# Layer 3's way back to its queries turned on TensorE, bias rows as products, and a different order around the choice

## The chip, the cores and the metric

The kernel runs on one core of one Trainium2 chip. Its time is the device time of one execution in microseconds, as the median of a few runs. The core has five engines with a queue of their own: TensorE (PE, with its weight loads as PEld), VectorE (DVE), ScalarE (ACT), GpSimd (POOL) and SyncE (SP), which issues most of the DMAs. Each works through its queue in order and waits on semaphores for the others.

## The reference

Four layers of gated cross-attention, each followed by a feed-forward part, on eight batches of 256 tokens with 128 features, in f32:

```python
x = x + tanh(g_xattn[l]) * L{l}_xattn(layernorm(x), ctx)      # l = 0 .. 3
x = x + tanh(g_ffn[l]) * L{l}_ffn(layernorm(x))
```

All attentions have 16 heads of 8 features. Layers 0 to 2 are full ones (2 causal). Layer 2's FFN is a mixture of 8 experts (2 per token) and a shared one. Layer 3 matters most here:

```python
q_norm = q / norm(q);  k_norm = k / norm(k)
mean_scores = einsum('bhqd,bhkd->bhqk', q_norm, k_norm).mean(-1)
_, top_idx = top_k(mean_scores, 51)                  # per head
q_sel = take_along_axis(q, top_idx)
attn = softmax(q_sel @ k.T / sqrt(8));  ctx_sel = attn @ v
context = zeros(...).at[bidx, hidx, top_idx].set(ctx_sel)
out = context.reshape(Bq, 256, 128) @ Wo.T + bo
```

So per head 51 of 256 queries attend, and their results go back to their places among 256. Layer 3's FFN quantizes its input to a grid of 6-bit numbers by blocks of 32, and multiplies by a quantized weight, plus a bias.

## The kernel before

The order of all work is written out by hand. A list of "beats" holds, for each beat, jobs in a fixed order (`beat(...)`) and jobs that `put` fits in by a rough cost per engine or `force` sets by number. At the end `plan_.run()` issues them beat by beat, so every engine's queue follows the beats. `one_bank()` hands out the eight banks of PSUM in turn: a new one waits until its last user eight banks ago is done.

Layers 0 to 2 interleave attention steps with the FFN of the layer before. The change touches three later places.

**The end of layer 2's attention** (the ten beats from `d`). The last batches are normed, routed to experts (`route2`: `logits`, `best`, `only`, `before_`, `index`, `label`, `send`) and scattered to DRAM by POOL. `shared_hidden` and `shared_project` (the shared expert, four pieces each per pair of batches) fill in. `shared_project(blk, 0)` first turns `cmb`, the weights of the experts ("codes"), into `cmbT` by four products (L1024) and a copy on ACT (L1028), and then uses it in a product of 8 rows (L1035) that adds the experts' biases. After these beats `tabulate` gives the table of tiles, SP fetches weights and rows, and 39 expert tiles follow (`tile_turn` L961, `tile_hidden` L975, `tile_project` L1001).

**The choice** (beats from `beats3b`). The experts' results are added (`combine`, L1058), each pair of batches is normed (`stats`, `first`, `steps_`, `apply`; four pairs, the first three with Newton steps on POOL, the last on DVE, `apply` L308 on ACT) and turned (`turn_norm`, L326/L327). `square_queries` (L1133, L1135) squares the projected queries. `lengths` (L1144, `reciprocal` L1148) and `cosines` (L1155, L1160 to L1162) of two pairs at a time give the rank numbers `sc` for all heads and batches at once. `choose` takes the 51 greatest of each row with seven rounds of `max`, numbers them 1 to 51 in `gt` (`order_`, L1199/L1200), sends `gt` to DRAM (`places3`, L1201), and `spread` turns it into `chosen` (L1207/L1208).

**Layer 3** (`PLACE3`). One beat per step `i`; each name in the list is issued for batch `i + k`:

- `one_hot` (L1258, DVE): a table of 128 x 1632, 1 where a query is the u-th chosen one; `gather` (L1283, PE) multiplies the projected queries (`query_rows`) by it.
- `scores3` (L1299), `maxima3` (L457, DVE), `lower3` (L1311, a copy on ACT and a DMA `k<-nT` L1316 of the negated maxima), `weights3` (L1325, exponentials on ACT L1332), `values3` (L1343), `turn3` (L1353 and three DVE operations): the softmax of the 51 queries of each head.
- `fetch_places` (L1249): two DMAs of 512 KB from `places3`, each row broadcast to 64 partitions; `one_hot_back` (L1253, DVE) compares the 128 x 2048 values with the lane's number. `spread3` (L1376, PE) multiplies the results by this table.
- `output` (`add_to_x`: L530 brings x into a bank by the identity, L532 adds the product, ACT copies it back, L535); the bias row `ob` is added by POOL (`bias`, `add_row` L331). `vals` adds the value bias in two POOL operations (L390).
- Layer norm (`stats` .. `apply`) with Newton steps on POOL (L265 to L268, `m` L298/L299), the grid FFN (`scales` .. `sized`, split over DVE and POOL), `turn_`, `out_` (again `add_to_x`, then the DMA out), with its bias row `frow` added by POOL (`add_row`). Batches 6 and 7 do these on DVE.

Of the kernel before, what the change touches and what calls it, by code (L numbers as in the profile page):

```python
# [88 lines left out]
def tile_gated_cross_attention_stack(ctx: ExitStack, tc: tile.TileContext, ins: dict, out: bass.AP):  # L89
# [182 lines left out]
    def layer_norm(bs, row=None, eng=None, out_eng=None, lag=2, wait=1):  # L272

        n = len(bs)
        eng = eng or G
        got = {}

        def stats(k):
            if k == 0:
                got["mv"] = tiny("mv", [P, 4, 2])[:, 0 : 2 * n, :]  # L280
            st, mv = tiny("st", [P, 2, 6]), got["mv"]
            for i in range(2):
                V.bn_stats(st[:, i, :], xs[:, 2 * bs[k] + i, :])
                V.bn_aggr(mv[:, 2 * k + i, :], st[:, i, :])

        def first():
            v = tiny("v", [P, 4])[:, 0 : 2 * n]
            V.tensor_scalar(v, got["mv"][:, :, 1], LN_EPS, None, ALU.add)
            got["y"] = *guess(v, 2 * n, f"ln{n}"), v

        def steps_():
            y, t_, v = got["y"]
            newton(y, t_, v, eng)
            m = tiny("m", [P, 4])[:, 0 : 2 * n]
            if eng is V:
                V.scalar_tensor_tensor(m, got["mv"][:, :, 0], -1.0, y, ALU.mult, ALU.mult)  # L296
            else:
                eng.tensor_tensor(m, got["mv"][:, :, 0], y, ALU.mult)  # L298
                eng.tensor_scalar(m, m, -1.0, 0.0, ALU.mult, ALU.add)  # L299
            got["m"] = m  # L300

        def apply(k):
            t = norm[bs[k]] = moe.tile([P, 2, ROW], F32, tag="xn", name="xn", bufs=8)
            for i in range(2):
                c = slice(2 * k + i, 2 * k + i + 1)
                o, x, y, m = t[:, i, 0:D], xs[:, 2 * bs[k] + i, :], got["y"][0][:, c], got["m"][:, c]
                if out_eng is A:
                    A.activation(o, x, AF.Identity, bias=m, scale=y)  # L308
                else:
                    eng.tensor_scalar(o, x, y, m, ALU.mult, ALU.add)  # L310

        e = "V" if eng is V else "G"
        todo = [(1, dict(V=0.7), stats, k) for k in range(n)]
        todo += [(1, dict(V=0.5), first), (1, {e: 2.8 if eng is G else 1.9}, steps_)]
        todo += [
            ((wait if eng is G else 1) if k == 0 else 1, dict(A=0.7) if out_eng is A else {e: 0.9}, apply, k) for k in range(n)
        ]
        todo += [(lag if k == 0 else 0, dict(T=0.45, A=0.37), turn_norm, b) for k, b in enumerate(bs)]
        if row is not None:
            todo += [(0, dict(G=0.73), add_row, b, row) for b in bs]  # L320
        return todo
# [55 lines left out]

    def vals(l, b):
        ps = one_bank()
        for c in range(2):  # L380
            nc.tensor.matmul(
                ps[:, c * P : (c + 1) * P], lhsT=ctxT[:, b * S + c * P : b * S + (c + 1) * P], rhs=wvo[:, l, 0, :],
                start=True, stop=True,
            )
# [3 lines left out]
        if l == NL - 1:  # L388
            for c in range(2):
                G.tensor_tensor(o[:, c], o[:, c], bv3.rearrange("p (h d) -> p h d", d=HD), ALU.add)  # L390
# [136 lines left out]
    def add_to_x(b, xT, w):  # L527

        px, xb = one_bank(), xs[:, 2 * b : 2 * b + 2, :].rearrange("p t d -> p (t d)")
        nc.tensor.matmul(px[:, 0:S], lhsT=ident, rhs=xb, start=True, stop=False)  # L530
        for c in range(2):
# [5 lines left out]
    def output3(b):  # L537
        add_to_x(b, cts.pop((NL - 1, b)), wvo[:, NL - 1, 1, :])
# [479 lines left out]

    def shared_project(blk, i):
        t, hT = 4 * blk + i, shared[blk]  # L1020
        if i == 0:
            ps = one_bank()
            for k in range(4):
                nc.tensor.matmul(  # L1024
                    ps[0:NE, k * P : (k + 1) * P], lhsT=cmb[:, 4 * blk + k, :], rhs=ident, start=True, stop=True
                )
            cT = work.tile([P, 512], F32, tag="sy", name="cmbT", bufs=2)[0:NE, :]
            A.copy(cT, ps[0:NE, :])  # L1028
            shared[blk, "c"] = cT
# [107 lines left out]
    def lengths(ms):  # L1137
# [3 lines left out]
        o, ps = slice(32 * ms[0], 32 * ms[0] + 64), one_bank()  # L1141
# [6 lines left out]
        V.reciprocal(rank3["sc"][o], ps[o, 0:S])  # L1148

    def cosines(ms):  # L1150

        o, ps = slice(32 * ms[0], 32 * ms[0] + 64), one_bank()
        for k in range(2):
            for m in ms:
# [3 lines left out]
                )  # L1158
        sc, size = rank3["sc"][o], rank3["size"][o]
# [4 lines left out]
    def choose():  # L1164
# [31 lines left out]
        def order_():  # L1196
# [4 lines left out]
            nc.sync.dma_start(out=places3[:, :], in_=gt)  # L1201
# [20 lines left out]
    places3 = dram.tile([P, S], F32, tag="places3", name="places3")  # L1222
# [3 lines left out]
    def area(b):  # L1226
# [4 lines left out]
            o[:, 256:512].rearrange("p (g s u) -> p g s u", g=2, s=2),  # L1231
        )

    def clear_area(r, i):
        q, a, u = area(r)
        if i == 0:
            G.memset(q, 0.0)
        else:
            G.memset(a, 0.0)
            G.memset(u, 1.0)  # L1240

    def fetch_places(b):
# [3 lines left out]
        o = a3[b, "back"] = a3["back"][:, b % 2].rearrange("p (k q) -> p k q", q=S)  # L1246
        src = places3[b * H : (b + 1) * H, :].rearrange("(k s) q -> s k q", s=2)
        for s in range(2):
            nc.sync.dma_start(out=o[64 * s : 64 * s + 64], in_=src[s].unsqueeze(0).to_broadcast([64, 8, S]))  # L1249

    def one_hot_back(b):
        o = a3[b, "back"]
        V.tensor_scalar(o, o, lane64, None, ALU.is_equal)  # L1253

    def one_hot(b):
# [5 lines left out]
        )  # L1261

# [10 lines left out]
    def gather(b):  # L1273
        q, a, _ = area(b)
        o = a3.pop((b, "to"))
# [59 lines left out]
    def values3(b):  # L1335
# [11 lines left out]
        A.copy(area(b)[2][:, :, :, 0:U], ps[:, 0 : 4 * U].rearrange("p (g s u) -> p g s u", g=2, s=2))  # L1347

    def turn3(b):
        u = area(b)[2]  # L1350
        pt = one_bank()
        for g in range(2):
            nc.tensor.transpose(pt[:, g * P : (g + 1) * P], u[:, g].rearrange("p s u -> p (s u)"), ident)  # L1353
        pt = pt[:, 0:S].rearrange("p (k e) -> p k e", e=32)
        rd, own = tiny("rd3", [P, 8]), tiny("own3", [P, 8, 2])
        V.reciprocal(rd, pt[:, :, HD])
        V.tensor_tensor(
            own, rd.unsqueeze(2).to_broadcast([P, 8, 2]), own_half.unsqueeze(1).to_broadcast([P, 8, 2]), ALU.mult
        )
        shape = [P, 8, 2, HD]  # L1360
        V.tensor_tensor(
            ctx3(b)[:, :, 0 : 2 * HD].rearrange("p k (s d) -> p k s d", s=2),
# [6 lines left out]
    def spread3(b):  # L1369
# [3 lines left out]
        for i in range(2):  # L1373
            for j in range(4):
                k = 2 * j + i
                nc.tensor.matmul(  # L1376
                    pt[strip(j), 0:S], lhsT=x[:, 32 * k - 16 * i : 32 * k - 16 * i + 32], rhs=back_[:, k, :],
# [80 lines left out]
    def ffn3(b, eng=None):  # L1458
# [9 lines left out]
        def out_():  # L1468
            xb = xs[:, 2 * b : 2 * b + 2, :]
            add_to_x(b, got["rT"], w3T)  # L1470
# [9 lines left out]
        (-1, "turn3"), (0, "lower3 bias"), (-2, "apply"), (2, "one_hot"), (1, "gather"), (-1, "spread3"), (1, "fetch_places"),  # L1480
        (0, "weights3"), (-1, "output"), (-4, "out_"), (-3, "off add_row"), (-2, "scales units_"), (0, "one_hot_back"), (-3, "lower_ sized"), (1, "scores3"),
        (-2, "step scale_"), (0, "values3"), (-1, "stats first steps_"), (-2, "near"), (1, "vals"),
# [64 lines left out]
    own_head = own2 = head_rows = u51 = lane64 = own_rows = own_half = bq3 = every = None  # L1547

    def more_constants():
        nonlocal prior, region, first, tiles, lane, token2, nowhere, taken, ident16, mask16, own_head, own2, head_rows  # L1550
        nonlocal u51, lane64, own_rows, own_half, bq3, every
# [25 lines left out]
        for m in range(NB // 2):  # L1577
# [3 lines left out]
        u51, lane64 = count("u51", [P, TOP_QUERIES], [[1, TOP_QUERIES]], 1), count("lane64", [P, 1], [[1, 1]], 1, 1)  # L1581
        upper = shaped("upper", [P, 1], 0.0, (None, [[0, 1]], ALU.is_ge, -64.0, 63, -1))
        G.tensor_tensor(lane64, lane64, upper, ALU.add)
        own_half = shaped(
            "own_half", [P, 2], 1.0, (lambda t: t[:, 0:1], [[0, 1]], ALU.is_ge, 0.0, 63, -1),
            (lambda t: t[:, 1:2], [[0, 1]], ALU.is_ge, 0.0, -64, 1),
# [78 lines left out]
    for base in (  # L1665
        (last(1),), (fill[0][0], last(3)), (fill[0][1], last(5)), (fill[0][2], last(7), fill[0][3]),
        ((keys, 3, 0), (keys, 3, 1)), ((keys, 3, 2),), (fill[0][4],), (fill[0][5],),
        ((keys, 3, 3), (square, 0), fill[0][6], (square, 1), fill[0][7], (squares, 0), fill[1][0]),
# [33 lines left out]
    for i in range(TILES + 2):  # L1702
# [20 lines left out]
        {p[2].__name__ + str(p[3] if p[2].__name__ in ("apply", "stats") else ""): p[2:] for p in layer_norm(pair, ob[:, 3, :], G if m in (0, 1, 2) else V, A)}  # L1723
# [16 lines left out]
    for base in (  # L1740
        [(take, b) for b in range(NB)] + h2 + joins(0, V), p2[0:2] + statistics(0), p2[2:4] + h3 + joins(1, V),
        statistics(1) + joins(2, V) + p3[0:2] + applied(0), turned_(0) + statistics(2) + p3[2:4] + applied(1) + [(square_queries, 0)],
        turned_(1) + joins(3, V) + [(square_queries, 1)], statistics(3), applied(2), turned_(2) + applied(3) + [(square_queries, 2)],
        [(lengths, (0, 1)), (cosines, (0, 1))], turned_(3) + [(square_queries, 3)],
        [(lengths, (2, 3)), (cosines, (2, 3))],
# [11 lines left out]
    for b in range(NB):  # L1757
        eng = G if b < 6 else V
        for p in last_norm((b,), frow[:, 1, :], eng, A) + ffn3(b, eng):
            what[p[2].__name__, b] = p[2:]  # L1760
        for f in (
            query_rows, one_hot, one_hot_back, fetch_places, gather, scores3, maxima3, lower3, weights3, values3, turn3, spread3
        ):
            what[f.__name__, b] = f, b
        what["bias", b] = add_row, b, ob[:, NL - 1, :]
        what["vals", b], what["output", b] = (vals, NL - 1, b), (output3, b)
    first = [(f, b) for b in range(2) for f in ("fetch_places", "query_rows", "one_hot")]
# [76 lines left out]
```

## Time and profile before

| | |
|---|---|
| median of 3 runs | 872.11 us (871.02 to 877.95) |
| the profiled execution's own time | 872.14 us |
| its span | 870.4 us |
| mean granted TensorE clock | 0.933 of full speed |
| busy PE, DVE, ACT, POOL | 776.4, 640.5, 444.3, 387.9 us |
| expert tiles | about 603 to 697 us of the span |
| `choose` and `spread` | about 732 to 743.6 us |
| layer 3's attention and FFN | 743.6 us to the end |

A line of the timeline gives start, length, engine, source line, operation, out<-in by the program's names, shapes (partitions x elements), how often, and in brackets the engine's idle time before it and what ended that. A line of the chain of waits gives start, length and what held the end up. An f32 product shows as two MATMULs, a transpose as one; PE's lengths overlap, so the spacing of starts tells what one costs in a stream.

### The profile page before, as it was taken

What the parts mean: (1) busy time and instruction counts of PE and PEld (TensorE: products, weight loads), DVE (VectorE), ACT (ScalarE), POOL (GpSimd) and SP (SyncE); (2) the same over time, 40 slices, a digit from 0 to 9 for tenths busy, and PEclk for the clock granted to TensorE, in tenths of its full rate; (3) what the DMA queues carried; (4) which work ended last, traced back from release to release, by engine and by line L of the source; (5) the groups of instructions that cost most, each with busy time, mean ns of one, the idle gap of its engine ahead of it and who ended that gap; (6) DMA issues with size and microseconds to landing.
All of it is one profiled execution on the core that took longest, in us unless ns stands there. A gap on an engine that the chain in (4) does not pass through costs nothing.

```text
span 870.4 us, 23085 instructions
## 1 busy us (share of the span) xinstructions
PE 776.4 (89%) x8682; PEld 555.2 (64%) x8682; DVE 640.5 (74%) x1972; ACT 444.3 (51%) x1111; POOL 387.9 (45%) x1022
## 2 busy tenths in 40 slices
PE   4999999999999999999999998859999995587775
PEld 2666667666766666666776676535998861465553
DVE  7978889898886578767656675746687576578886
ACT  2567777777776522222665563635455542354442
POOL 3425478777433205022522235574455540048771
PEclk7999999999999999999999996978999996698885
DMA  4314333222220000010100100324576330553430
GB/s 121 103 52 101 86 86 93 62 66 64 65 56 3 1 1 1 2 24 2 27 15 15 27 10 21 110 80 126 145 201 184 94 96 0 104 100 75 87 63 24
DMA packets 59758, 56.40 MB, mean 65 GB/s; under 512 B 7112, under 2 KB 48912, under 8 KB 59648
## 3 DMA queue, kind: packets, MB, share of 16 engines
q1 hardware_dynamic: 56944, 50.06, 22.9%
q0 software_dynamic: 2272, 4.72, 1.5%
q8 instruction: 69, 1.13, 0.6%
q14 instruction: 41, 0.34, 0.1%
q10 hardware_dynamic: 432, 0.15, 0.1%
HBM read 31.99 MB, written 15.16 MB: 54 GB/s over the span
## 4 chain that ended last, share of the span: by engine, by line
PE 66%; DVE 22%; ACT 4%; issue 4%; POOL 3%; DMA 2%; another core or an unknown queue 0%; SPq 0%; DVEq 0%; ACTq 0%
PE one L405 17%; PE one L485 8%; DVE nm L457 7%; PE one L745 4%; PE one L734 4%; PE one L735 4%; PE one L975 4%; PE one L1001 4%; PE one L342 3%; PE one L394 2%; PE one L1032 2%; PE one L521 1%; ACT e L460 1%; PE one L1014 1%; DVE back L1253 1%
## 5 line engine op out<-in xcount | busy, mean ns | idle before, releaser
L457 DVE TENSOR_REDUCE nm<-one 128x2 f32<-128x512 f32 (+1 forms) x416 | 240.6, 642 | 85.3 <-PE one L394 42.9
L460 ACT ACTIVATE e<-one 128x512 f32<-128x512 f32 (+1 forms) x384 | 185.9, 566 | 59.9 <-PE one L405 58.5
L405 PE MATMUL one<-q,k 32*128 32x256 f32 (+1 forms) x1536 | 191.1, 381 | 5.4 <-issue 1.6
L405 PE MATMUL one<-k,q 32*128 32x256 f32 (+1 forms) x1536 | 185.3, 387 | 3.2 <-DMA q<-proj 3.2
L405 PEld LDWEIGHTS one<-k,q 32*128 32x128 f32 x1536 | 133.3, 193 | 36.1 <-issue 15.2
L405 PEld LDWEIGHTS one<-q,k 32*128 32x128 f32 x1536 | 139.1, 189 | 16.2 <-issue 5.4
L485 PE MATMUL one<-e,vaug 128*32 128x256 f32 (+1 forms) x1536 | 87.3, 369 | 1.0 <-ACT e L460 0.9
L411 POOL TENSOR_SCALAR_AFFINE_SELECT e<-e 128x1024 f32<-128x1024 f32 x32 | 35.0, 1094 | 96.2 <-ACT e L460 80.4
L265 POOL TENSOR_TENSOR t_ln<-y_ln 128x2 f32<-128x2 f32 (+1 forms) x105 | 21.4, 204 | 104.0 <-DVE y_ln L255 98.5
L485 PEld LDWEIGHTS one<-e,vaug 128*32 128x32 f32 x1536 | 45.2, 111 | 33.8 <-DVE nm L457 5.1
L980 ACT ACTIVATE h<-one,tb 128x128 f32<-128x128 f32 x156 | 44.6, 370 | 41.2 <-PE one L975 36.9
L785 POOL DMA_INDIRECT done<-y,back_to x39 | 39.5, 1014 | 48.2 <-DVE xT L963 27.5
L737 ACT ACTIVATE act<-one 128x512 f32<-128x512 f32 x40 | 23.9, 597 | 61.0 <-PE one L734 56.0
L745 PEld LDWEIGHTS one<-ffn,act 128*128 128x128 f32 x320 | 41.2, 192 | 16.7 <-issue 14.1
L738 DVE TENSOR_TENSOR act<-act,one 128x512 f32<-128x512 f32 x40 | 27.4, 685 | 25.8 <-PE one L735 18.7
L491 ACT COPY u<-one 128x256 f32<-128x256 f32 x48 | 17.9, 374 | 48.9 <-PE one L485 48.4
L975 PE MATMUL one<-xT,k 128*128 128x128 f32 x312 | 41.5, 276 | 1.0 <-DVE xT L963 1.0
L308 ACT ACTIVATE xn<-xs,m,y_ln 128x128 f32<-128x128 f32 x64 | 27.7, 487 | 26.9 <-DVE m L296 17.2
L745 PE MATMUL one<-ffn,act 128*128 128x128 f32 x320 | 41.4, 275 | 0.0
L734 PE MATMUL one<-xnT,ffn 128*128 128x512 f32 x80 | 41.3, 598 | 0.0
L1001 PE MATMUL one<-w2all,h 128*128 x312 | 41.2, 276 | 0.0
L735 PE MATMUL one<-xnT,ffn 128*128 128x512 f32 x80 | 40.9, 592 | 0.0
(346 smaller groups left out, 1571.1 us busy)
## 6 DMA issues: line engine op xcount, KB each, us to landing
k<-in_w_dram SPq DMA_DIRECT2D x39, 256.0 KB
sent<-zero SPq DMA_DIRECT2D x34, 264.0 KB
back<-places SPq DMA_DIRECT2D x16, 512.0 KB
k<-proj SPq DMA_DIRECT2D x24, 128.0 KB
q<-proj SPq DMA_DIRECT2D x48, 64.0 KB
xt<-sent SPq DMA_DIRECT2D x39, 66.0 KB
w2all<-in_w_dram SPq DMA_DIRECT2D x4, 512.0 KB
yt<-done SPq DMA_DIRECT2D x8, 256.0 KB
```

Source lines behind the costliest of these rows:

```text
L405: nc.tensor.matmul(o, lhsT=a, rhs=r, start=alone_ or s == 0, stop=alone_)
L411: G.affine_select(d, d, pattern=[[0, 8], [1, P]], compare_op=ALU.is_ge, fill=0.0, base=0, channel_multiplier=-1)
L457: V.tensor_reduce(nm, ps.rearrange("p (s k) -> p s k", s=2), AX.X, ALU.max, negate=True)
L460: A.activation(e, ps[:, 0 : 2 * w].rearrange("p (s q) -> p s q", s=2), AF.Exp, scale=SCALE)
L485: nc.tensor.matmul(ps[strip(j), q0:S], lhsT=va[:, at : at + 32], rhs=e[:, c, j, s, 0 : S - q0], start=c == 0 and s == 0, stop=c == 1 and s ...
L734: nc.tensor.matmul(pa, lhsT=wa, rhs=toks, start=True, stop=True)
L735: nc.tensor.matmul(pb, lhsT=wb, rhs=toks, start=True, stop=True)
L745: nc.tensor.matmul(py[:, i * P : (i + 1) * P], lhsT=a[:, i * P : (i + 1) * P], rhs=w, start=n == 0, stop=n == len(ws) - 1,)
L785: i = G.indirect_dma_start(out=dst[:, :], out_offset=bass.IndirectOffsetOnAxis(ap=rows_, axis=0), in_=src, in_offset=None)
L975: nc.tensor.matmul(ps[:, ch * P : (ch + 1) * P], lhsT=wa[:, ch * P : (ch + 1) * P], rhs=turned[i][0], start=True, stop=True)
L980: A.activation(h[:, ch, :], ps[:, ch * P : (ch + 1) * P], AF.Gelu, bias=plan["tb"][:, i, ch : ch + 1])
L1001: nc.tensor.matmul(ps[:, 0:D], lhsT=h[:, ch, :], rhs=wb[:, ch, :], start=ch == 0, stop=ch == NCH - 1)
```

## The change

1. `places3`, `fetch_places` and `one_hot_back` go. `turn_places(b, i)` makes the table of the way back from the gathering one: per batch 16 transposes of 128 x 102 on PE, into four banks, and four copies of 102 x 512 on ACT. `turn3` and `spread3` work on 102 partitions in place of 128, and `one_hot` moves in `PLACE3` from the front to between `step scale_` and `stats`, with the transposes in two halves around `scores3`. Before the loop only batch 0's `query_rows` and `one_hot` are made.
2. The three bias rows of layer 3 are products of a row of ones (one partition) with the row, accumulated into the bank that is filled anyway (`row_to`): in `vals`, `output3` and `out_`. POOL's additions go.
3. The codes of the first shared block (`shared_codes(0)`) are turned three beats earlier; pieces of the shared expert move by one beat or within one.
4. `lengths` and `cosines` are split from `inverse` and `ranked`; the first pairs' products stand ahead of the last turnings, and the last pair's second batch is normed on DVE (`vector_too`).

```diff
-                if out_eng is A:
+                if out_eng is A and k not in vector_too:
                     A.activation(o, x, AF.Identity, bias=m, scale=y)
...
+    def row_to(ps, row, start=False):
+        nc.tensor.matmul(
+            ps[:, 0:S].rearrange("p (c d) -> p c d", c=2), lhsT=ones[0:1, 0:P],
+            rhs=row[0:1].unsqueeze(1).to_broadcast([1, 2, D]), start=start, stop=False,
+        )
     def vals(l, b):
+        last = l == NL - 1
+        if last:
+            row_to(ps, bv3, True)
...
-        if l == NL - 1:
-            for c in range(2):
-                G.tensor_tensor(o[:, c], o[:, c], bv3.rearrange("p (h d) -> p h d", d=HD), ALU.add)
...
-    def add_to_x(b, xT, w):
+    def add_to_x(b, xT, w, row):
         nc.tensor.matmul(px[:, 0:S], lhsT=ident, rhs=xb, start=True, stop=False)
+        row_to(px, row)
...
+    def shared_codes(blk):
...
-        if i == 0:
+        if i == 0 and (blk, "c") not in shared:
+            shared_codes(blk)
...
-            nc.sync.dma_start(out=places3[:, :], in_=gt)
...
-    def fetch_places(b):
...
-        for s in range(2):
-            nc.sync.dma_start(out=o[64 * s : 64 * s + 64], in_=src[s].unsqueeze(0).to_broadcast([64, 8, S]))
-    def one_hot_back(b):
-        V.tensor_scalar(o, o, lane64, None, ALU.is_equal)
+    def turn_places(b, i):
+        o, t = a3[b, "to"], a3["back"][0 : 2 * U, b % 2].rearrange("p (k q) -> p k q", q=S)
+        for k in range(4 * i, 4 * i + 4, 2):
+            ps = one_bank()
+            for m in range(2):
+                for c in range(2):
+                    at = (2 * m + c) * P
+                    nc.tensor.transpose(
+                        ps[0 : 2 * U, at : at + P],
+                        o[:, c, 2 * (k + m) : 2 * (k + m) + 2, :].rearrange("p s u -> p (s u)"), ident,
+                    )
+            A.copy(t[:, k : k + 2, :].rearrange("p k q -> p (k q)"), ps[0 : 2 * U, :])
...
     PLACE3 = (
-        (-1, "turn3"), (0, "lower3 bias"), (-2, "apply"), (2, "one_hot"), (1, "gather"), (-1, "spread3"), (1, "fetch_places"),
-        (0, "weights3"), (-1, "output"), (-4, "out_"), (-3, "off add_row"), (-2, "scales units_"), (0, "one_hot_back"), (-3, "lower_ sized"), (1, "scores3"),
-        (-2, "step scale_"), (0, "values3"), (-1, "stats first steps_"), (-2, "near"), (1, "vals"),
+        (-1, "turn3"), (0, "lower3"), (-2, "apply"), (1, "gather"), (-1, "spread3"),
+        (0, "weights3"), (-1, "output"), (-4, "out_"), (-3, "off"), (-2, "scales units_"), (1, "turn_places0"), (-3, "lower_ sized"), (1, "scores3"),
+        (-2, "step scale_"), (0, "values3"), (1, "turn_places1"), (2, "one_hot"), (-1, "stats first steps_"), (-2, "near"), (1, "vals"),
         (2, "query_rows"), (-3, "turn_"), (1, "maxima3"),
     )
...
-        (last(1),), (fill[0][0], last(3)), (fill[0][1], last(5)), (fill[0][2], last(7), fill[0][3]),
-        ((keys, 3, 0), (keys, 3, 1)), ((keys, 3, 2),), (fill[0][4],), (fill[0][5],),
-        ((keys, 3, 3), (square, 0), fill[0][6], (square, 1), fill[0][7], (squares, 0), fill[1][0]),
+        (last(1),), (fill[0][0], last(3)), (fill[0][1], last(5)), (fill[0][2], (shared_codes, 0), last(7), fill[0][3]),
+        ((keys, 3, 0), (keys, 3, 1)), ((keys, 3, 2),), (fill[0][4], fill[0][5]), (fill[0][6],),
+        ((keys, 3, 3), (square, 0), (square, 1), fill[0][7], fill[1][0], (squares, 0)),
...
-        turned_(1) + joins(3, V) + [(square_queries, 1)], statistics(3), applied(2), turned_(2) + applied(3) + [(square_queries, 2)],
-        [(lengths, (0, 1)), (cosines, (0, 1))], turned_(3) + [(square_queries, 3)],
-        [(lengths, (2, 3)), (cosines, (2, 3))],
+        turned_(1) + joins(3, V) + [(square_queries, 1)], statistics(3) + applied(2), [(lengths, (0, 1)), (cosines, (0, 1))],
+        applied(3) + turned_(2) + turned_(3) + [(inverse, (0, 1)), (ranked, (0, 1)), (square_queries, 2), (square_queries, 3)],
+        [(lengths, (2, 3)), (cosines, (2, 3)), (inverse, (2, 3)), (ranked, (2, 3))],
...
-    first = [(f, b) for b in range(2) for f in ("fetch_places", "query_rows", "one_hot")]
+    first = [("query_rows", 0), ("one_hot", 0)]
```

## The prediction

> **What bounds the kernel now.** I read the page first, then the stretches from 560 us on (the layers before them are cut into the same instructions by both kernels), then the timeline there.
>
> ```profile
> PE 776.4 (89%) x8682; PEld 555.2 (64%) x8682; DVE 640.5 (74%) x1972; ACT 444.3 (51%) x1111; POOL 387.9 (45%) x1022
> ```
>
> TensorE (PE) is 89% busy overall, but not where the change lies. Layer 3 works on one batch after the other, some 13 us each. In two of those stretches (length, then PE, PEld, DVE, ACT and POOL busy, granted clock, DMA share, GB/s):
>
> ```profile
> 786.30:799.54 13.24, 11.07 (x230) 8.33 (x220) 11.54 (x26) 5.86 (x18) 10.68 (x24) 0.74 0.41 82
> 799.54:812.80 13.26, 10.73 (x237) 8.29 (x228) 11.57 (x27) 6.14 (x19) 10.70 (x24) 0.87 0.42 91
> ```
>
> VectorE (DVE) does 11.6 of 13.26 us and GpSimd (POOL) 10.7, so the pace is set by the two together. The timeline of one batch shows how (start, length, engine, instruction, idle time before it):
>
> ```profile
> 799.54 1.89 DVE L1258 TENSOR_TENSOR to<-chosen,u 128x1632 f32<-128x1632 f32 x1
> 799.80 1.68 POOL L298 TENSOR_TENSOR m<-mv,y_ln 128x2 f32<-128x2 f32 x1
> 801.80 0.88 ACT L308 ACTIVATE xn<-xs,m,y_ln 128x128 f32<-128x128 f32 x2 [2.09 <-POOL m L299]
> 802.71 0.42 DVE L1400 TENSOR_REDUCE q_scl<-xn 128x8 f32<-128x256 f32 x1 [1.28 <-ACT xn L308]
> 803.90 1.83 DVE L1253 TENSOR_SCALAR back<-back,lane 128x2048 f32<-128x2048 f32 x1
> ```
>
> POOL's tiny `m`, elsewhere 0.20 us, lasts 1.68 and ends with `one_hot` (L1258): the two get in each other's way. The ring is: y_ln on DVE (796.39), Newton steps on POOL, `m`, `xn` on ACT, L1400 at 802.71 (6.3 later), then 6.9 of DVE work with L1253 in it to the next y_ln at 809.64. PE meanwhile:
>
> ```profile
> 812.28 0.28 PE L1311 MATMUL one<-ident,nm 128*8 128x128 f32 x1 [1.29 <-DVE nm L457]
> ...
> 813.30 1.07 PE L1376 MATMUL one<-back,zero 128*32 128x256 f32 x16
> 814.76 1.15 PE L1325 MATMUL one<-k,keys 32*128 32x102 f32 x32 [0.39 <-DMA k<-nT]
> 815.85 0.70 PE L530 MATMUL one<-xs,ident 128*128 128x256 f32 x2
> 817.37 0.71 PE L532 MATMUL one<-wvo,cT 128*128 128x128 f32 x4 [0.83 <-ACT cT L1381]
> 817.92 0.60 PE L530 MATMUL one<-xs,ident 128*128 128x256 f32 x2
> 818.36 0.61 PE L532 MATMUL one<-w3T,rT 128*128 128x128 f32 x4
> 818.89 1.15 PE L1299 MATMUL one<-keys,k 32*128 32x256 f32 x16
> ...
> 823.90 0.41 PE L1353 MATMUL one<-ident,k 128*128 128x128 f32 x2 [1.70 <-DVE nm L457]
> 825.61 0.38 PE L1311 MATMUL one<-ident,nm 128*8 128x128 f32 x1 [1.29 <-DVE nm L457]
> ```
>
> From start to start the pieces of this batch come to 8.8 us at nearly full clock (1.0 to L1376, 1.0, 1.1, 0.6, 0.55, 0.45, 0.55, 1.1, then 0.85 values, 0.55 `vals`, 0.45 queries, two times 0.3 turning); the rest of 13.3 is waiting. So PE has 4.5 us to spare per batch.
>
> Two places ahead of the loop also hold PE:
>
> ```profile
> 582.69 0.79 PE L1035 MATMUL one<-b,cmbT 8*128 8x128 f32 x2 [7.83 <-ACT cmbT L1028]
> ...
> 711.24 1.16 PE L1032 MATMUL one<-w,hT 128*128 128x128 f32 x8
> 712.33 0.48 PE L1035 MATMUL one<-b,cmbT 8*128 8x128 f32 x2
> ```
>
> ```profile
> 719.26 1.65 ACT L308 ACTIVATE xn<-xs,m,y_ln 128x128 f32<-128x128 f32 x4
> 721.42 1.92 PE L1144 MATMUL one<-qsq,head_sum 128*32 128x256 f32 x8
> 724.98 1.01 PE L326 MATMUL one<-ident,xn 128*128 128x128 f32 x4
> ```
>
> At 574.9 PE stops for 7.8 us until ACT, busy with the labels of batch 6, comes to copy the codes. At 721 the last pair's normed rows are ready, but their turning (724.98) stands behind `lengths` and `cosines` of the first pairs.
>
> **The change, part by part.** Times are set against the profiled execution: 872.14 us, of which 870.4 is the span. The median of the runs is 872.11, so the sum carries over.
>
> *Codes ahead.* The copy now stands before ACT's labels, so batch 7's turning no longer waits for L1035. ACT still copies the labels first (to 581.6) and one projection (0.68), then xnT: 582.2 in place of 584.14, 1.9 earlier. DVE's choice of experts and the table follow it. One `shared_project` (1.7 us, L1032 and L1035 from 591.86) also leaves the stretch before the first tile turns at 602.96; what that gives is limited by the rows' DMA, issued at 598.88. Ends 1.9 and 3.4; I take **-2.5**. The codes' four products (1.0 us of PE) now stand ahead of batch 7's last product; DVE reads that only at 570.79 and not before 568.8, so they are covered, and would cost 1.0 otherwise.
>
> *Choice.* `lengths` and `cosines` of the first pairs (1.85 + 1.7 us) run while DVE does the last statistics, and two of the last four `xn` go to DVE (0.3 each instead of 0.41 in ACT's row). The last turning then waits for `xn` (719.8) and not for 724.98. With the four turns, copies and two L1133 behind each other, `lengths` of the last pairs ends near 725.2 at full clock (729.4 now), 726.7 at the clock of L1144's row: -2.7 to -4.2, **-3.4**. The `reciprocal` of the first pairs (1.75) still ends before the second begins.
>
> *Tables.* Removed per batch: L1253 (1.82 on DVE), two DMAs of 512 KB on SP's queue, two `add_row` (0.73 each) and two `vaug` additions (0.43 each) on POOL. Added on PE: 16 transposes and three one-row products; on ACT four copies of 102x512, bounded by 0.56 (8x512 copy) and 0.69 (128x512 activation), so 2.4, with 6 of 13 us used so far: covered.
>
> A transpose: the pairs of L1353 and L1464 show 0.11 us of spacing (L1353's row: 0.41 for two, 0.27 of it the last one's own latency); 16 make 1.8. The price is bounded above by that latency, 0.27.
>
> A one-row product of 256 columns: L530's spacing (817.92 to 818.36) gives 0.44. The nearest row with few partitions is L1035: 0.41 for 128 columns where full products take 0.22, and the L1032 group behind it takes 1.09 where it takes 0.89 at 613.33. So 0.4 more: 0.83, and three make 2.5. 0.44 is the lower end. *TensorEngine Tiling (Array Packing)* of the Trainium skill, Tiling Modes, Key Properties, says that changing the tiling mode drains TensorE. By it each of the three products pays on both sides; without it the sum below would be 5.9 us lower (the first rival). L1035's rows agree with it.
>
> PE per full batch: 8.8 + 1.8 + 2.5 + 0.4 (weights wait for `nT`'s DMA) = **13.5**. The ring on DVE, POOL and ACT: L1253's 1.8 leaves the second part and `one_hot` (1.9) enters it, between `step` and the statistics, 7.1; in the first part `m` is no longer held up (-1.5): 4.9. Together **12.0**. `one_hot` now holds POOL's `scale_` instead, which is needed only after statistics and `first` (1.9 us later). So PE takes over the pace, 0.2 above today's.
>
> Batch by batch (from L1311 to L1311; today 12.7, 9.6, 12.0, 13.25, 13.25, 13.3, 11.85): before the first, PE does 16 transposes and one product more, partly under the wait for `k`: +0.7. Batch 0 loses the wait below, but PE's longer queue takes most of it: -0.9.
>
> ```profile
> 752.18 4.80 DMA k<-nT
> ```
>
> (4.80 behind the tables' transfers; 1.65 at 764.88.) Batch 1, which has little else: 11.3, +1.7. Batch 2: 11.4, -0.6. Batch 3, no output of the FFN yet: PE 11.7, the ring 12.0, -1.25. Batches 4 and 5: +0.2, +0.1. Batch 6, whose `one_hot` and queries are gone: 13.0, +1.1. Batch 7 has no transposes left and L1253 is gone, 1.8, and 0.5 of the lead that DVE has from batch 6: -2.3. At the end two products stand on the chain where the clock is low (L530's second piece takes 0.86 to 1.0 at 865.27 and 851.94): +2.0; the POOL additions that they replace were hidden there.
>
> Sum: -2.5 - 3.4 + 0.7 - 0.9 + 1.7 - 0.6 - 1.25 + 0.2 + 0.1 + 1.1 - 2.3 + 2.0 = -5.15. **867.0 us.**
>
> **Rivals.**
>
> *The ring sets the pace (0.26).* The one-row products pay no switch (0.44), so PE needs 12.3 per full batch. Some 15 products count on the path, 0.39 each: 5.9 less, **861.1**. For it: they are accumulations into a bank already open. Against it: L1035 is one too, and pays.
>
> *The gains ahead of the loop are swallowed (0.2).* The expert stage starts when rows arrive, not when PE is free, and `choose` when DVE is done: half of 5.9 is lost and the loop costs one more: **871**. For it: between 577.44 and 579.43 DVE waits for something that the trace calls unknown, which the change leaves.
>
> *Transposes don't overlap (0.1).* Each costs its latency, 0.27, not 0.11: 2.6 us more per batch, on PE's queue, which is the bound from 0.1 each on. Batches -1 to 6, one of them half covered: 7 x 2.4 = 17 us: **884**, slower. Against it: four L326 at 709.35 let the next product start at 709.84. *TensorE: Matmul & The Clock Gate* (Part 4: PE-mode transpose) gives about 275 ns for one in a kernel; the row's 0.27 is the same figure, but as latency, not as spacing. By that figure as a spacing the sum would be this rival's.
>
> That the change does not do what it says I see no case for: the transposes and products stand in the changed queue.
>
> **How the numbers follow.** The forecast has 0.44, with 863.5 to 870.5 as its own range. The ends of the terms (start 1.9 to 3.4, choice 2.7 to 4.2, products 0.44 to 0.83) and the first two rivals span 860 to 872; I reach to 876 for part of the third. 1%, 8.7 us, is about what a measurement can tell from no change here (its runs reach from 871.02 to 877.95). Below 863.4: the first rival and a little of the forecast, 0.31. Above 880.8: 0.09. Between: 0.60.
>
> **What would show it.** Right: L1253 gone; PE over 12.5 of 13.5 us busy in the full batches at a clock near 1.0; POOL's `m` at 0.2; the pace near 13.5 and unchanged; `nT`'s DMA below 2.5 us in batch 0; no wait of 7.8 us for `cmbT`; the first tile turned near 600.5, `chosen` near 737.5. Wrong: batches of 12 us with PE idle before L457's releases (then the products are cheap), or above 15 (then the transposes are dear); `chosen` at 742 or later.

## The result, and the profile after

The changed kernel takes 868.78 us (median of 20 runs, 863.34 to 872.79) and the kernel before 872.02 (20 runs): ratio 0.996, 95% interval 0.9943 to 0.9978. In a later set of runs, beside the kernel before on the same chip, it was 0.9938 (0.9922 to 0.9954). It is a little faster, by less than 1%, as forecast. The profiled run took 870.73 us with a span of 867.9.

Its page, first line (to be held against PE 89%, DVE 74% and POOL 45% before):

```profile
PE 805.0 (93%) x8858; PEld 571.9 (66%) x8858; DVE 622.5 (72%) x1966; ACT 460.4 (53%) x1141; POOL 363.5 (42%) x984
```

The full batches 4 and 5, by stretch (length, then PE, PEld, DVE, ACT and POOL busy, granted clock, DMA share, GB/s):

```profile
792.98:806.08 13.10, 12.73 (x242) 9.42 (x241) 9.23 (x24) 8.48 (x24) 8.94 (x23) 1.00 0.05 13
806.08:819.18 13.10, 12.72 (x242) 9.40 (x241) 9.23 (x24) 8.35 (x24) 7.71 (x19) 1.00 0.05 13
```

They are 13.10 long where they were 13.25, but another engine fills them: TensorE works for 12.7 us where it worked for 10.7 to 11.1, VectorE has gone from 11.6 to 9.2. TensorE's timeline of the second of them:

```profile
806.08 0.39 PE L1329 MATMUL one<-ident,nm 128*8 128x128 f32 x2
...
808.52 1.15 PE L1343 MATMUL one<-k,keys 32*128 32x102 f32 x32 [0.38 <-DMA k<-nT]
809.61 0.70 PE L537 MATMUL one<-xs,ident 128*128 128x256 f32 x2
810.24 0.69 PE L380 MATMUL one<-ob,ones 1*128 1x256 f32 x2
810.86 0.71 PE L540 MATMUL one<-wvo,cT 128*128 128x128 f32 x4
811.41 0.60 PE L537 MATMUL one<-xs,ident 128*128 128x256 f32 x2
811.93 0.69 PE L380 MATMUL one<-frow,ones 1*128 1x256 f32 x2
812.56 0.71 PE L540 MATMUL one<-w3T,rT 128*128 128x128 f32 x4
813.11 1.04 PE L1274 MATMUL one<-ident,to 128*102 128x128 f32 x8
814.07 1.15 PE L1317 MATMUL one<-keys,k 32*128 32x256 f32 x16
```

L380 is `row_to`, L1274 the transposes of `turn_places`, L1329 is `lower3` (L1311 before). The only wait is 0.38 us for `nT`'s DMA; no piece waits for VectorE any more. Eight transposes take 0.96 to 1.02 us from start to start, 0.12 to 0.13 each.

The batches in the order of the prediction (first `lower3` to the next, and at last to `spread3` of batch 7): 10.0, 11.3, 11.2, 11.4, 13.1, 13.1, 16.3, 10.9. The 16.3 is a disturbance of this one trace: from 824.6 to 831.5 us the granted clock was 0.5, and a second trace of the same kernel (below) has 13.2 there. That second trace stands for batch 6 and for the length of the loop in what follows.

### The profile page after: what moved, and what is told of

It is laid out like the page before. It is cut to its first block, busy times and chain, and to the rows that moved or that the text cites. A ratio compares the mean times of both kernels' runs of the same rounds, so it can differ in the third digit from the quotient of the medians.

```text
span 867.9 us, 23365 instructions
## 1 busy us (share of the span) xinstructions
PE 805.0 (93%) x8858; PEld 571.9 (66%) x8858; DVE 622.5 (72%) x1966; ACT 460.4 (53%) x1141; POOL 363.5 (42%) x984
## 4 chain that ended last, share of the span: by engine, by line
PE 72%; DVE 16%; DMA 4%; ACT 3%; issue 2%; POOL 1%; another core or an unknown queue 1%; SPq 0%; DVEq 0%; ACTq 0%; POOLq 0%
PE one L412 17%; PE one L492 8%; DVE nm L464 6%; PE one L753 4%; PE one L742 4%; PE one L743 4%; PE one L983 4%; PE one L1009 3%; PE one L342 3%; PE one L1274 2%; PE one L380 2%; PE one L401 2%; PE one L1043 1%; PE one L540 1%; DMA k<-nT 1%
## 5 line engine op out<-in xcount | busy, mean ns | idle before, releaser
L464 DVE TENSOR_REDUCE nm<-one 128x2 f32<-128x512 f32 (+1 forms) x416 | 240.5, 640 | 91.2 <-PE one L401 42.9
L412 PEld LDWEIGHTS one<-q,k 32*128 32x128 f32 x1536 | 138.7, 189 | 16.1 <-issue 5.1
L492 PE MATMUL one<-e,vaug 128*32 128x256 f32 (+1 forms) x1536 | 87.2, 369 | 1.0 <-ACT e L467 0.9
L492 PEld LDWEIGHTS one<-e,vaug 128*32 128x32 f32 x1536 | 45.2, 111 | 33.8 <-DVE nm L464 5.1
L283 DVE BATCH_NORM_STATS2 st<-xs 128x6 f32<-128x128 f32 x128 | 34.6, 270 | 7.4 <-ACT xs L543 6.9
```

Source lines behind the costliest of these rows:

```text
L412: nc.tensor.matmul(o, lhsT=a, rhs=r, start=alone_ or s == 0, stop=alone_)
L464: V.tensor_reduce(nm, ps.rearrange("p (s k) -> p s k", s=2), AX.X, ALU.max, negate=True)
L492: nc.tensor.matmul(ps[strip(j), q0:S], lhsT=va[:, at : at + 32], rhs=e[:, c, j, s, 0 : S - q0], start=c == 0 and s == 0, stop=c == 1 and s ...
```

## The experiments

One reading goes through all of them. The stretch from layer 2's end to the first expert tile varied by up to 12 us between traces whose code is the same up to there, so a trace is cut at two marks: the start of layer 2's last values product (L492, L485 before) and the end of the copy into `chosen`. What lies behind the second mark repeats to a few tenths where the clock is the same. The runs were made on different chips, on which the kernel before has medians from 866.9 to 875.3 us, so times are compared as ratios to it on the same chip. In us:

| kernel | layer 2's last values to chosen | chosen to first lower3 | a full batch | chosen to end of span | time to before, with interval |
|---|---|---|---|---|---|
| before | 184.9 | 7.9 | 13.25 | 126.8 | |
| changed, first trace | 180.4 | 10.0 | 13.10 | 128.9 | 0.996 (0.9943 to 0.9978) |
| changed, second trace | 175.2 | 9.2 | 13.12 | 126.0 | 0.9938 (0.9922 to 0.9954) |
| biases on GpSimd | 184.0 | 9.0 | 12.36 | 120.0 | 0.9884 (0.9847 to 0.992) |
| codes not ahead | 187.5 | 9.7 | 13.1 | 126.3 | 0.9982 (0.9952 to 1.0012) |
| choice in the old order | 184.6 | 9.4 | 13.1 | 126.3 | 0.9986 (0.9956 to 1.0016) |
| row through the identity | 179.2 | 10.1 | 11.93 | 119.0 | 0.9845 (0.9805 to 0.9884) |
| the same, weights later | 178.9 | 10.1 | 11.55 | 120.8 | 0.9882 (0.9845 to 0.9919) |
| before, plus products | 187.1 | 9.1 | 12.55 | 125.2 | 1.0002 (0.9971 to 1.0033) |
| row in two halves | 182.2 | 9.2 | 13.1 | 127.3 | one run, 871.73 us |
| one_hot behind statistics | 180.0 | 9.0 | 12.12 | 123.3 | 0.9908 (0.9879 to 0.9938) |
| tables alone | 182.5 | 9.1 | 12.37 | 120.1 | 0.9927 (0.9909 to 0.9945) |
| identity, out_ first | 175.9 | 8.9 | 11.64 | 118.4 | 0.9854 (0.9831 to 0.9877) |

My theory going in was the prediction's: TensorE sets the pace, a one-row product costs it some 0.8 us, and the earlier choice reaches the end. The rivals were a pace set by VectorE and GpSimd, and gains ahead of the loop that are lost on the way.

**Biases on GpSimd.** The one-row products undone, the rest of the change kept.

```diff
-            row_to(ps, bv3, True)
...
+                G.tensor_tensor(o[:, c], o[:, c], bv3.rearrange("p (h d) -> p h d", d=HD), ALU.add)
...
-        row_to(px, row)
...
-        (-1, "turn3"), (0, "lower3"), (-2, "apply"), (1, "gather"), (-1, "spread3"),
+        (-1, "turn3"), (0, "lower3 bias"), (-2, "apply"), (1, "gather"), (-1, "spread3"),
...
-        (0, "weights3"), (-1, "output"), (-4, "out_"), (-3, "off"), ...
+        (0, "weights3"), (-1, "output"), (-4, "out_"), (-3, "off add_row"), ...
...
```

> The changed kernel with its three bias rows per batch added on GpSimd again (as before the change) and no one-row products. Theory (TensorE sets the pace of the loop and each product costs it 0.6 to 0.8 us): a full batch, 13.1 us in the changed kernel, loses 2.1 us of TensorE work and falls to the ring of VectorE, ScalarE and GpSimd, 11.5 to 12.0; the batches before it lose 0.6 to 1.3 each, the end about 1.2. Together 5 to 7 us: 862 to 864 where the changed kernel has 868.8. Rival (GpSimd's additions, 2.3 us per batch, lengthen the ring by as much as the products cost TensorE): full batches stay at 12.8 to 13.2, TensorE waits 2 us in each, and only the end gains 1: 867 to 869.

Measured: full batches 12.36, 120.0 us behind the choice in place of 126.0. A full batch and, from the waits of two batches, the longest of TensorE:

```profile
796.18:808.54 12.36, 10.86 (x234) 8.63 (x234) 9.93 (x25) 8.38 (x22) 9.83 (x24) 1.00 0.05 14
```

```profile
PE one L1283 <- DVE nm L464: 2.4, 2, 1.6
```

TensorE is 10.9 busy of 12.36 and waits for VectorE again: the ring is back as the bound, at 12.36 (0.4 above the top of what I had written). The bias products, which the change brought in, cost 6 us of what its tables gained.

**Row through the identity.** The row lies on all 128 partitions, so the identity brings it in as well as a row of ones does.

```diff
-            ps[:, 0:S].rearrange("p (c d) -> p c d", c=2), lhsT=ones[0:1, 0:P],
-            rhs=row[0:1].unsqueeze(1).to_broadcast([1, 2, D]), start=start, stop=False,
+            ps[:, 0:S].rearrange("p (c d) -> p c d", c=2), lhsT=ident,
+            rhs=row.unsqueeze(1).to_broadcast([P, 2, D]), start=start, stop=False,
```

> The changed kernel with each bias row brought in by the 128-partition identity and the row on all partitions, in place of a one-partition product of ones and the row; the same 256 columns and the same sum. Theory (the one-row product's extra is the change between a one-partition and a full product, on either side): start to start falls from 0.62 to 0.44-0.53 on both sides, a full batch from 13.1 to 12.4-12.6, the end by 0.5; together 3 to 4 us, 865. Rival (the extra belongs to the 256 columns and the weights' load, whatever the partitions): start to start stays at 0.62, 868.8.

The same pieces in its timeline:

```profile
796.19 0.70 PE L537 MATMUL one<-xs,ident 128*128 128x256 f32 x2
796.73 0.59 PE L380 MATMUL one<-ob,ident 128*128 128x256 f32 x2
797.16 0.61 PE L540 MATMUL one<-wvo,cT 128*128 128x128 f32 x4
797.60 0.60 PE L537 MATMUL one<-xs,ident 128*128 128x256 f32 x2
```

Against the changed kernel, the start-to-start times fall three times for one product: into it from 0.63 to 0.54, out of it from 0.62 to 0.43, and of L540 behind it from 0.55 to 0.44. That is 0.09 + 0.19 + 0.11 = 0.39, and the batch agrees: (13.10 - 11.93) / 3 = 0.39. I had expected a batch of 12.4 to 12.6 because I had looked for the extra on the two sides only. A change of the stationary operand by itself is not what costs: L380 and L540 have different ones here too (the identity and `cT`), and start 0.43 apart. The identity is the largest single gain of all: 7 us behind the choice.

**Row in two halves.** Two of the three one-row products cut into two of 128 columns.

```diff
...
+            for c in range(2):
+                nc.tensor.matmul(
+                    ps[:, c * P : (c + 1) * P], lhsT=ones[0:1, 0:P], rhs=row[0:1], start=False, stop=False
+                )
...
```

> The changed kernel with two of the three one-row products (output and out_) cut into two of 128 columns each, one behind the other; the same columns in all. Theory (the extra 0.39 is paid where a one-partition product follows or precedes a full one, not inside it): the two halves cost 0.22 each and the extra once, full batches stay at 13.1 to 13.3. Rival (every one-partition product costs 0.39 more, whatever stands beside it): full batches 13.8 to 14.0.

```profile
800.05 0.71 PE L382 MATMUL one<-ob,ones 1*128 1x128 f32 x4
800.69 0.71 PE L546 MATMUL one<-wvo,cT 128*128 128x128 f32 x4
```

(L382 is `row_to` here, L546 the product behind it.) 0.64 from start to start for the two halves, 0.62 for the whole; full batches 13.12 and 13.16. A second one-partition product behind a first costs its columns and nothing more: the extra belongs to the change from one kind to the other. *TensorEngine Tiling (Array Packing)* of the Trainium skill, Tiling Modes, Key Properties, says that a change of the tiling mode drains TensorE. These two runs agree, with 0.39 us per product there and back; that a one-partition product is such a change is my reading, for the traces name no mode.

**Before, plus products.** The kernel before with `row_to` in place of GpSimd's additions and nothing else (the same edit as above, the other way round).

> The kernel before with the three one-row products per batch in place of GpSimd's additions, and nothing else changed. Theory (before, TensorE has 4.5 us to spare per batch, so that three products of 0.83 cost nothing in the loop, and GpSimd's relief takes a little from the ring): full batches 12.8 to 13.3 as before (13.25), TensorE 2.5 us busier in each, the end 1 to 2 longer; the copy of the chosen places to the end of the span 126 to 129 us (126.8 before). Rival (the products stand on the chain from spread3 to the statistics, which closes the ring): full batches 14 or more, 131 or more from the chosen places to the end.

```profile
789.69:802.21 12.52, 10.49 (x217) 7.77 (x217) 10.82 (x26) 5.74 (x17) 7.57 (x20) 0.89 0.43 87
802.21:814.78 12.57, 12.33 (x225) 8.71 (x225) 10.88 (x26) 6.16 (x18) 7.56 (x20) 0.86 0.45 97
```

The same products that cost 6 us in the changed kernel cost nothing here: GpSimd falls from 10.7 to 7.6 and the batches are 0.7 shorter, a little below what I expected; the time is unchanged (1.0002). An operation's price is that of the stage it lands in. They were free beside the old tables, and the tables turned on TensorE took away the room that made them free.

**Tables alone.** Biases, codes and choice all undone.

> The changed kernel with its biases on GpSimd, the codes and the choice in the old order: of the change only the turned tables are left. Theory (each part counts for itself): full batches 12.36 as in the run with the biases on GpSimd, the chosen places to the end 120 us (126.8 before), the first tile to the chosen places 140 to 141 as before, the time 6 to 7 below the kernel before: ratio 0.992. Rival (the parts need each other, the tables' transposes being in the way of an order that was made for the tables from DRAM): 122 or more from the chosen places to the end, ratio 0.996 or more.

120.1 us behind the choice and batches of 12.37, as expected; ratio 0.9927, beside 0.9938 (0.9922 to 0.9954) of the whole change on the same chip. One part of four is worth as much as all four: what codes and choice gain, the bias products give back.

**Codes not ahead, choice in the old order.** Each of the two undone by itself.

```diff
-        (fill[0][2], (shared_codes, 0), last(7), fill[0][3])
+        (fill[0][2], last(7), fill[0][3])
...
-        (fill[0][4], fill[0][5]), (fill[0][6],),
+        (fill[0][4],), (fill[0][5],),
...
-        statistics(3) + applied(2), [(lengths, (0, 1)), (cosines, (0, 1))],
+        statistics(3), applied(2), turned_(2) + applied(3) + [(square_queries, 2)],
+        [(lengths, (0, 1)), (inverse, (0, 1)), (cosines, (0, 1)), (ranked, (0, 1))], turned_(3) + [(square_queries, 3)],
```

> The changed kernel with the codes copied inside the first shared projection again, and the shared pieces where they stood. Theory (the codes gain only the 1.0 us that the first tile's turning moved between the two traces): first tile turned at 602.5 to 603.2 in place of 601.9, time 1.0 higher, 869.8. Rival (the 2.5 us of the prediction are there, but hidden in the changed kernel's one trace by a stall that comes and goes): first tile at 604 or later, 871.3. On the stall (VectorE's addition to batch 7 at 576.50, 7.6 us behind an unknown cause; 570.79 before the change): if it belongs to the new order, it is gone here; if it belongs to the place in the program or to chance, it may be there.

> The changed kernel with the last normalisations, turnings, lengths and cosines in the old order. Theory (the 3.5 us between the two traces come from this part alone and reach the end whole): the copy of the chosen places ends near 742.5 in place of 739.0, time 3.5 higher, 872.3. Rival (the head of the loop waits for something else, so that an earlier choice is partly lost): chosen near 742.5 but the time only 1 to 2 higher, 870 to 871, with the first lower3 less late than chosen.

Both leave the loop alone (126.3 us behind the choice). Both lose about 0.2% against the changed kernel's first ratio, 0.996, with overlapping intervals, and 0.4 to 0.5% against its second, 0.9938, where the intervals just meet or just miss each other; the second was taken on another chip, so the times alone don't settle it. The choice can be read between two other marks, from the first tile's turning to `chosen`: the four traces with the old order take 138.1 to 141.4 us, mean 140.2, the nine with the new one 135.6 to 139.2, mean 136.9. That is 3.3 us between the means, though the two ranges meet, where the two traces of the prediction's kernels gave 3.5. The codes cannot be read from one trace, because of waits like these (all engines, changed kernel, first trace):

```profile
575.07 0.57 ACT L1034 COPY cmbT<-one 8x512 f32<-8x512 f32 x1 [5.54 <-remote]
...
576.50 0.48 DVE L532 SCALAR_TENSOR_TENSOR xs<-one,tg,xs 128x256 f32<-128x256 f32 x1 [7.65 <-remote]
...
577.04 2.44 PE L1043 MATMUL one<-w,hT 128*128 128x128 f32 x8 [4.98 <-issue]
```

ScalarE and VectorE stand for 5 to 8 us although the products that they read had ended at 568; "remote" is a cause that the trace doesn't know. The wait moves: in the run with the biases on GpSimd, whose code is the same there, L532 waits for nothing unknown, but ScalarE's xnT stands for 4.8, and the stretch from the last values to the first tile is 4.8 us longer. Without the codes ahead the first tile turned at 611.5, later than either of my two values, but this is inside what comes and goes. From the last values to the first tile, the nine traces with the codes ahead take 36.5 to 48.1 us, mean 42.6, the four without 41.7 to 51.2, mean 46.5: earlier with them, but inside the spread. Of the eight traces with codes and choice in the new order, the two that come to the first tile soonest (36.5 and 36.8) take the longest from there to `chosen` (138.7 and 139.2), which suggests that a part of an early start is lost again. Over both stretches the eight take 179.5 us on the mean between the marks of the table (175.2 to 184.0), the three with neither 184.8 (182.5 to 187.1): 5.3 us for the two together.

**The changed kernel again.**

> The changed kernel once more, for a second trace of it beside the next two. Theory (the low clock of 824 to 831 us in its first trace, and the wait of 7.6 us on VectorE at 568.9, come by chance and not from the order): batch 6 takes 13.3 us in place of 16.3, the chosen places to the end 126.3 in place of 128.9, and the stretch from the last attention of layer 2 to the first tile's turning is anywhere from 42 to 48 us. Rival (they belong to the kernel): 16.3 and 128.9 again.

```profile
810.67:823.84 13.17, 12.28 (x238) 8.96 (x237) 7.38 (x23) 8.01 (x23) 6.26 (x19) 1.00 0.05 13
```

Batch 6 takes 13.17 at a clock of 1.0, where the first trace had 16.33, and there is no wait at L532: both came by chance. The stretch from the last values to the first tile was 36.5, outside the 42 to 48 that I gave it.

**Three attempts to do better.** *Weights later:* the identity, and `turn_places0` ahead of `weights3`, so that TensorE works while `nT`'s DMA lands.

```diff
-        (0, "weights3"), (-1, "output"), (-4, "out_"), (-3, "off"), (-2, "scales units_"), (1, "turn_places0"), ...
+        (1, "turn_places0"), (0, "weights3"), (-1, "output"), (-4, "out_"), (-3, "off"), (-2, "scales units_"), ...
```

> The run with the rows through the identity, and in the order written out by hand the first half of the next batch's transposes put ahead of this batch's weights product, so that TensorE works while nT's DMA lands (0.46 us of waiting per batch there). Theory (in that run TensorE and the ring of VectorE, GpSimd and ScalarE both need 11.9 us): TensorE's wait goes, but full batches stay at 11.8 to 12.0; only batches 0 to 2 lose 0.3 to 0.4 each; 861 beside the 861.5 of the run with the identity. Rival (TensorE alone sets the pace): full batches 11.5, 858.5.

Here the rival was right. The batch has no gap left:

```profile
790.23:801.78 11.55, 11.55 (x240) 9.67 (x240) 9.06 (x24) 7.87 (x22) 7.76 (x20) 1.00 0.05 15
```

TensorE alone set the pace, and the ring needs 11.55 or less. The 1.8 us that it lost behind the choice against the identity alone lie in batch 0, 11.9 against 9.4: the values there waited 0.70 us for ScalarE, which now copies the tables first, and from 753.5 to 756.9 us the granted clock was 0.5.

*One_hot behind statistics:* besides, `one_hot` moved behind "stats first steps_", to shorten a ring that, as it turned out, was not the bound, and batch 1's query rows ahead of the loop.

> The run with the identity and the weights later, and besides one_hot behind the statistics and their first step in place of ahead of them, and batch 1's query rows ahead of the loop again. Theory (with one_hot, 1.85 us, out of VectorE's stretch between step and y_ln, the ring falls to about 10.1 and TensorE, which no longer waits for nT, sets the pace at 11.5): full batches 11.4 to 11.6, the copy of the chosen places to the first lower3 9.5 to 10.0 in place of 10.4; 3 us below the run with the identity, 858. Rival (one_hot now holds near and the maxima by 1.85 us, which release the next lower3): full batches 12 or more, 861 or more.

```profile
802.21 1.85 DVE L1262 TENSOR_TENSOR to<-chosen,u 128x1632 f32<-128x1632 f32 x1
803.98 0.28 DVE L1443 TENSOR_SCALAR q_r<-q_y 128x256 f32<-128x256 f32 x1
804.18 2.47 DVE L464 TENSOR_REDUCE nm<-one 128x2 f32<-128x512 f32 x4
```

The rival was right again: L464, which releases the next `lower3`, starts behind `one_hot` and ends at 806.65, 0.06 ahead of `lower3`, and the batches take 12.12. Moving the same 1.85 us a few places in one queue cost 0.57 per batch against the run before.

*Out_ first:* the identity, and only `out_` ahead of `weights3`.

> The run with the rows through the identity, and out_ of the fourth batch back put ahead of this batch's weights product, in place of the transposes, so that only the batches with an out_ (4 to 7) cover nT's DMA. Theory (TensorE sets the pace there): batches 0 to 3 as in the run with the identity (9.4, 10.5, 10.5, 11.3), full batches 11.5 in place of 11.93, the chosen places to the end 117.5 to 118.5 in place of 119.05, the time 1 below it. Rival (out_'s copy now stands ahead of the weights' exponentials on ScalarE and delays the values): full batches 11.9 or more, the same time.

```profile
784.36:795.96 11.60, 11.60 (x240) 9.74 (x241) 9.07 (x24) 8.02 (x22) 7.81 (x20) 1.00 0.05 14
795.96:807.64 11.68, 11.68 (x241) 9.87 (x240) 9.13 (x24) 8.36 (x24) 7.79 (x21) 1.00 0.05 15
```

118.4 us behind the choice, the least of all, and the early batches stay at 9.4, 10.5, 10.5 and 11.3. Its ratio, 0.9854, is not to be told from that of the identity alone, 0.9845, on another chip. Either is some 1.5% faster than the kernel before and about 1% faster than the changed one.

## Why the prediction was right, step by step

**The total.** Forecast 867.0, measured 868.78 as a median and 870.73 in the profiled run; 3.2 us of that run are the half clock in batch 6. The range and the likeliest case held. Some terms missed in both directions, by up to 1.8 us (batch 0), and they nearly cancel; that much of the agreement is luck.

**What bounds the loop: right.** The price of a one-row product, 0.83, was taken from L1035's row, and is 0.44 + 0.39 in the runs. TensorE's batch was forecast at 13.5 and is 13.1: transposes 2.0 (1.8 forecast), products 2.5 (2.5), waiting 0.38 (0.4), which leaves 8.2 for the old pieces, forecast at 8.8. The first rival (products at 0.44) is what the identity gave: it forecast 861.1, a ratio of 0.987, for a measured 0.9845 (0.9805 to 0.9884). TensorE still set the pace there, not the ring of VectorE, GpSimd and ScalarE, as the batch of 11.55 without a gap shows. The third rival (transposes of 0.27) fell with the 0.12 to 0.13 that the timeline shows; the figure of about 275 ns that the Trainium skill gives (*TensorE: Matmul & The Clock Gate*, Part 4: PE-mode transpose; there for bf16) holds here as a latency (0.27) and not as a spacing. The ring was forecast at 12.0 without GpSimd's additions; it needs 11.55 at most, and 12.36 with them; batch 3, forecast at the ring's 12.0, took 11.4.

**Codes and choice: right in sum, not apart.** -5.9 forecast (-2.5 and -3.4), -5.3 over all traces, 3.3 of it the choice. On one chip the tables alone are 5.9 us shorter behind the choice than the whole change but only 0.9 us faster (859.82 and 860.68), so codes and choice are worth some 5 us there too. Both speak against the second rival (half of it lost), but with traces that spread over 9 us they don't exclude it. The wait of 7.8 us for `cmbT` is gone, the first tile turned at 601.9 in the first trace (600.5 forecast) and `chosen` was copied by 739.0 (737.5). Of the codes alone only the sign is likely.

**Ahead of the first batch: too small.** +0.7 forecast, +2.1 and +1.3 in the two traces. The failed step is the clock: I costed the transposes at full clock, where the chain shows them at half.

```profile
742.64 1.88 PE one L1274 x8
744.52 1.88 PE one L1317 x16
```

The granted clock was 0.5 until 746.1 us, 7.1 behind `chosen`; before, until 746.2, which was 2.7 behind it. TensorE had stood for 12.3 us ahead of `chosen` in both. In the eleven traces with the new order of layer 3 the term goes with the moment at which the clock came back: 8.9 us where that was 4.8 behind `chosen`, 9.2 at 5.4, 9.7 at 6.4 and 10.1 at 7.8. In the old order it is 7.9 at 2.7, and 9.1 in the run with the products added to the kernel before, where the clock was at half all the way. So at least 1 us of the +2.1 is the clock's timing, which differs between traces of one code (7.1 and 5.4 for the changed kernel). TensorE stood a second time, for 1.59 us while `one_hot` ran (0.74 before), since batch 1's query rows, which filled half of that gap, had moved into the loop. This gap is not shown to hold the clock back: the run with `one_hot` behind the statistics closes it to 0.74 and has the clock back at 4.9, and five runs with 1.59 have it back at 4.8 to 5.4.

**Batch 0: too small a gain.** -0.9 forecast, -2.7 measured (12.7 to 10.0). `nT`'s DMA took 1.71 us in place of 4.80, as forecast (below 2.5); what I set against it, TensorE's longer queue, lay in the time that was waited before.

```profile
749.79 1.71 DMA k<-nT
```

**The other batches.** +1.6, -0.8, -1.9, -0.2, -0.2 for batches 1 to 5 (forecast +1.7, -0.6, -1.25, +0.2, +0.1); batch 6 +1.3 in the second trace (forecast +1.1); batch 7 -1.7 (-2.3). GpSimd's `m` is back at 0.20 us, and `scale_`, now held up by `one_hot`, lasts 2.21 with no one waiting for the difference. **The end:** 20.4 us before, 21.5 and 22.5 after: +1.1 and +2.2 for a forecast of +2.0.

## What to carry to other kernels

Price an added operation in the stage where it will run after the whole change, not in the one where it runs now: the same three products cost nothing beside the old tables and 6 us beside the new. When a change of several parts moves the time little, undo each part alone; here the tables gained 6.7 us behind the choice, codes and choice some 5 us before that, and the bias products took 6 back. And before a small operand is brought in through a partial tile, look whether the full one that is already loaded does the same.

## What the runs showed of the hardware

A matmul with one contracted partition between full ones costs 0.39 us beyond its columns, spread over three start-to-start times: 0.09 into it, 0.19 out of it and 0.11 on the product behind. Two such matmuls in a row pay it once. A full matmul behind the 32-partition ones of L1343 shows a like extra: 0.54 us to the next start, where one behind a full matmul takes 0.44 (L537 in the run with the identity).

The granted clock is full or half, and in all thirteen traces every stretch at one of the two, but for the first and last of a trace, lasts a whole multiple of 3.41 us (753.5 to 756.9 in one, 824.6 to 831.5 in another). Half-clock stretches come and go in one and the same code: one of 6.8 us after a wait of 0.86 us in batch 6 of the changed kernel's first trace, none after 0.89 at the same place in its second; one of 3.4 us after a wait of 0.70 in the run with the weights later, none after 1.27 in batch 0 of the run with the identity. The Trainium skill (*TensorE: Matmul & The Clock Gate*, Part 1) says that the gate watches activity in a window that runs freely, so that the same kernel can meet it at another phase; the traces agree with that, with 3.41 us as the step in which the clock changes.

What holds ScalarE and VectorE for 5 to 8 us near 570 us, in some traces and not in others, stays open.
